# Adding up a state space model's states one step later on TensorE

## The chip, the cores and the metric

The kernel runs on one core of one Trainium2 chip. Five engines of that core work side by side, each through its own queue in order: TensorE (PE in the profile, with PEld for its weight loads), VectorE (DVE), ScalarE (ACT), GpSimd (POOL) and SyncE (SP). ACT, SP and POOL also issue DMAs from their queues. Engines wait for each other on semaphores. The metric is the device time in microseconds of one execution; lower is better. Before the change the median of six runs was 1602.23 us (1597.44 to 1605.59).

## The reference, cut to what matters

Two layers act on 8 sequences of 512 tokens with 128 channels. Each layer is `x + s * silu(g)`, where `s` and `g` are two models that read the same normalised input and don't need each other. In the first layer `s` is a state space model and `g` a mixture of 24 experts; in the second `s` is an attention with 8 heads and `g` a mixture of 128 experts.

The part that matters here is the state space model:

```
deltaA  = exp(dt[..., None] * A)                 # A: 256 channels x 16 states
deltaBx = dt[..., None] * Bm[:, :, None, :] * x[..., None]
h = dA * h + dBx                                  # over the 512 tokens
y = einsum('bdn,bn->bd', h, C)                    # added up over the 16 states
y = (y + x * D) * silu(z)
```

and beside it the first mixture: 24 experts of 128 to 512 to 128 channels, with a normalisation of the summed hidden rows between the two products.

## The kernel before, in words

Everything is in fp32. A sequence of the state space model (`b`, eight of them) has its 256 channels in two halves of 128 partitions and its 512 tokens along the free axis. `front(b)` makes the inputs (convolution, `dt`, `B`, `C`) in two pieces; `scan(b, ...)` goes through the 16 states two at a time, so a sequence has 8 steps and the model 64; `back(b, yt)` does the output projection and a small MLP in three pieces.

One step of `scan` does the following for its two states (lines 597 to 636). ACT issues two DMAs that spread `B` and `C` over the partitions (`bb`, `cb`, lines 600 and 601, two buffers each). For each half, ACT makes `da = exp(dt * A)` for two states (line 606, two buffers), DVE multiplies `u = bb * dx` for both states at once (line 608), runs two scans along the tokens in place (line 610), and multiplies by `cb` (line 611). The tile `u` has four buffers, so two steps' worth. Then PE adds the states up: sixteen transposes by the identity (line 632) accumulate the two halves' two states, four token tiles each, into `py`, a PSUM tile with one buffer that lasts the whole sequence. A sequence's `py` is opened at its first step by the products of the `x * D` term (line 621), and the previous sequence's `py` is read just before by `gated` on DVE (`yt = py * zs`, line 652), which `turn()` calls.

The model is a Python generator that yields after each step; other parts of the program call `step()` to place the next step between their own pieces. One step stands ahead of the first mixture. The mixture has three stages. In `expert1(e)` (24 times) POOL gathers an expert's rows in three chunks, PE transposes them (line 450), ACT copies them out, PE adds a bias product and the expert's product (lines 456 and 457), ACT scales the result out of PSUM (line 458), and SP stores it. `between()` (16 times) gathers the pairs of hidden rows, sums and normalises them, mostly on POOL, DVE and ACT, and folds the attention's weights on PE beside it. `expert2(e)` (24 times) gathers again, transposes (line 521), and multiplies back to 128 channels (lines 524 and 526). A counter `due` spreads 11, 6 and 14 steps of the model over these three stages: it grows by 11/24, 6/16 or 14/24 after each piece, and a step is placed whenever it exceeds 0.5. The remaining 32 steps stand beside the attention of the second layer for sequences 0 to 5, 28 of them spread evenly over its 48 heads. After that come the last heads and the second mixture, without the model.

This is the order in which the program is written. Each engine's own queue is not quite in this order: the framework plans the order of every queue when the program is built, from its own estimate of when inputs are ready, and an earlier line goes first among those that it takes to be ready. On the chip a queue's order is fixed, and an instruction whose input is late holds everything behind it on its engine. `follows(later, earlier)` (line 119) adds an edge for this planning that says which of two instructions on one engine goes first; it costs no instruction and no semaphore.

Of the kernel before, what the change touches and what calls it, by code (L numbers as in the profile page):

```python
# [8 lines left out]
F32 = mybir.dt.float32  # L9
# [11 lines left out]
P = 128  # L21
B, L, D = 8, 512, 128
NJ = L // P
NTOK = B * L
NTT = NTOK // P
DI, DS, DTR, DFF = 256, 16, 8, 512
# [3 lines left out]
CP = 128  # L30
# [17 lines left out]
def tile_kernel(ctx: ExitStack, tc: tile.TileContext, t: dict, out: bass.AP):  # L48
    nc = tc.nc
    V, S, G, T, Q = nc.vector, nc.scalar, nc.gpsimd, nc.tensor, nc.sync  # L50
# [11 lines left out]
    ident = const.tile([P, P], F32, name="ident")  # L62
# [36 lines left out]
    def bc(ap, shape):  # L99
        return ap.to_broadcast(list(shape))  # L100
# [48 lines left out]
    def pool(stack, name, bufs, side, **more):  # L149
        return stack.enter_context(tc.tile_pool(name=name, bufs=bufs, side=side, **more))  # L150
# [6 lines left out]
    ps_y = pool(ssm, "ps_y", 1, "left", space=PSUM)  # L157
# [184 lines left out]
    ddiag = w0.tile([P, 2, P], F32, name="ddiag")  # L342
# [100 lines left out]
    def expert1(e, w):  # L443

        we = w(e)
        px = ps_e.tile([P, SLOTS], F32, name="px", tag="pe")
        for c, r in enumerate(SROWS):
            xg = me.tile([CP, D], F32, name="xg", bufs=8)
            gather(xg[:r], xn_dram, inv[:r, c, e : e + 1])
            T.transpose(px[:, c * CP : c * CP + r], xg[:r], ident[:r, :r])  # L450
        xT = me.tile([P, SLOTS], F32, name="xTe", tag="xTe")
        S.copy(xT, px)
        hs = me.tile([CP, SG, DH], F32, name="hs", tag="big", bufs=4)
        for c, r in enumerate(SROWS):
            ph = ps_e.tile([CP, DH], F32, name="ph", tag="pe")
            T.matmul(ph[:r], chosen(e, r), bias[:, 0:DH], start=True, stop=False)
            T.matmul(ph[:r], xT[:, c * CP : c * CP + r], we, start=False, stop=True)
            S.activation(hs[:r, c, :], ph[:r], AF.Copy, scale=wsl[:r, c, e : e + 1])
        store(hs_dram, e, hs)

    def between():

# [49 lines left out]
    def expert2(e, w):  # L512
        we = w(e)
        po = ps_e.tile([CP, SG, D], F32, name="po", tag="pe")
        os = me.tile([CP, SG, D], F32, name="os", tag="o")
        hg = me.tile([CP, SG, DH], F32, name="hg", tag="big", bufs=4)
        for c, r in enumerate(SROWS):
            gather(hg[:r, c, :], hid_dram, inv[:r, c, e : e + 1])
            pt = ps_e.tile([P, NJ, CP], F32, name="pht", tag="pe")
            for f in range(NJ):  # L520
                T.transpose(pt[:, f, :r], hg[:r, c, f * P : (f + 1) * P], ident[:r, :r])  # L521
            hT = me.tile([P, NJ, CP], F32, name="hgT", tag="xTe")
            S.activation(hT[:, :, :r], pt[:, :, :r], AF.Relu)  # L523
            T.matmul(po[:r, c, :], chosen(e, r), bias[:, DH:], start=True, stop=False)
            for f in range(NJ):
                T.matmul(po[:r, c, :], hT[:, f, :r], we[:, f, :], start=False, stop=(f == NJ - 1))  # L526
            S.activation(os[:r, c, :], po[:r, c, :], AF.Copy, scale=wsl[:r, c, e : e + 1])
        store(os_dram, e, os)

    def fetch(b):  # L530

# [59 lines left out]

    NC = 2

    def scan(b, xs, dt, dx, turn):


        for n0 in range(0, DS, NC):
            bb = ms.tile([P, NC, L], F32, name="bb")
            cb = ms.tile([P, NC, L], F32, name="cb")
            S.dma_start(bb, xd_dram[b][DTR + n0 : DTR + n0 + NC, :].partition_broadcast(P))  # L600
            S.dma_start(cb, xd_dram[b][DTR + DS + n0 : DTR + DS + n0 + NC, :].partition_broadcast(P))
            us = []
            for hf in range(2):
                da = ms.tile([P, NC, L], F32, name="da")
                for j in range(NC):
                    S.activation(da[:, j, :], dt[:, hf, :], AF.Exp, scale=a_neg[:, hf, n0 + j : n0 + j + 1])  # L606
                u = ms.tile([P, NC, L], F32, name="u", bufs=4)
                V.tensor_tensor(u, bb, bc(dx[:, hf : hf + 1, :], (P, NC, L)), ALU.mult)  # L608
                for j in range(NC):
                    V.tensor_tensor_scan(u[:, j, :], da[:, j, :], u[:, j, :], 0.0, ALU.mult, ALU.add)  # L610
                V.tensor_tensor(u, u, cb, ALU.mult)  # L611
                us.append(u)
            if n0 == 0:
                turn()

                py = ps_y.tile([P, NJ, DI], F32, name="py")
                for i in range(NJ):
                    for hf in range(2):  # L620
                        m = T.matmul(
                            py[:, i, hf * P : (hf + 1) * P], xs[:, hf, i * P : (i + 1) * P], ddiag[:, hf, :],
                            start=(i % 2 == 0 and hf == 0), stop=False, skip_group_check=True,
                        )
                        if i % 2 == 0 and hf == 0:
                            first = m
                        else:
                            follows(m, first)
            for hf in range(2):
                for j in range(NC):  # L630
                    for i in range(NJ):
                        T.matmul(  # L632
                            py[:, i, hf * P : (hf + 1) * P], us[hf][:, j, i * P : (i + 1) * P], ident,
                            is_transpose=True, start=False, stop=(n0 + j == DS - 1), skip_group_check=True,
                        )
            yield py

    def gate(xT):

# [368 lines left out]
    def step():  # L1008

        nonlocal taken  # L1010
        if taken < NSTEP:
            next(model_steps)
            taken += 1

    def model():


        for state in front(0):
            pass
        ending = iter(())  # L1020
        py = zs = None
        for b in range(B):
            xT, xs, dt, dx = state
            yts = []

            def turn():
                if b > 0:
                    yts.append(gated(py, zs))

            coming = front(b + 1) if b + 1 < B else iter(())  # L1030
            steps_b = scan(b, xs, dt, dx, turn)
# [11 lines left out]
            py, zs = pyb, zsb  # L1043
        for _ in back(B - 1, gated(py, zs)):
            pass

    NSTEP = B * DS // NC
    model_steps = model()
    taken = 0


    def mixture():
        w = weights((P, DH), t["W1"])
        for e in range(E0):
            expert1(e, w)
            yield 11, E0
        w = weights((P, NJ, D), t["W2"])
        w(0)
        for _ in between():
            yield 6, NTT // 2  # L1060
        for e in range(E0):
            expert2(e, w)
            yield 14, E0
# [3 lines left out]
    for n, of in mixture():  # L1067
        due += n / of
        while due > 0.5:
            step()  # L1070
            due -= 1.0
    moe.close()


# [56 lines left out]
    last = Attention(at, m_qk, w_vo, (ps_x, "px"), (ps_q, "pq"), (ps_s, "ps"), (ps_t, "pt"), (ps_o, "po"))  # L1131
# [95 lines left out]
```

## Time and profile before

| what | us |
|---|---|
| median of six runs | 1602.23 |
| the profiled execution, whole | 1593.88 |
| its span in the profile | 1592.2 |
| busy in the span: DVE | 1242.6 |
| busy in the span: PE | 1232.8 |
| busy in the span: ACT | 975.4 |
| busy in the span: POOL | 603.8 |
| PE's transposes of the states, line 632: busy | 165.2 (1024 of them, 302 ns each) |
| PE idle just before them, until a state's last product on DVE | 127.3 |

The stages follow each other in time, and in the profiled execution they lie about so: the first experts' stage from 95 to 288 us, the stage between from 288 to 433, the second experts' stage from 433 to 653, the turn to the second layer up to 742, attention beside the model up to 1323, and the rest.

Busy times are read against the span of a stage, not of the whole: an engine with the same share over the whole span can be full in one stage and nearly idle in another. An idle time in the profile is put down to the instruction in front of which the engine sat, and to what ended it. `PEclk` is the clock granted to TensorE as a share of the full one.

### The profile page before, as it was taken

The page shows a single profiled execution, that of the slowest core. Times are in us where ns is not written, and L with a number is a line of the kernel's source. Part 1 is how long each engine was busy: PE and PEld are TensorE (multiplying, and loading weights), DVE is VectorE, ACT ScalarE, POOL GpSimd, SP SyncE. Part 2 cuts the span into 40 slices and gives each one's busy share as a digit, 9 for nine tenths or more (in the row PEclk, how much of TensorE's full clock was granted, in tenths as well). Part 3 has the DMA queues.
Part 4 walks back from the last instruction along what each step waited for, and adds up shares of the span by engine and source line. Part 5 has one row for each costly group of instructions (what it writes and reads, how often), then busy time and mean ns, then how long its engine had stood idle before and what let it go on. Part 6 is the DMA issues. An engine that isn't in the chain of part 4 may idle for free.

```text
span 1592.2 us, 20596 instructions
## 1 busy us (share of the span) xinstructions
PE 1232.8 (77%) x6793; PEld 869.3 (55%) x6793; DVE 1242.6 (78%) x2759; ACT 975.4 (61%) x1726; POOL 603.8 (38%) x504
## 2 busy tenths in 40 slices
PE   6888889322579888547878989989889898899854
PEld 4644455222367776524556656766557576467533
DVE  5639775698946858769999999999899996465454
ACT  5146667577747677456766858667587675542442
POOL 1247552665154443573503560043260402010455
PEclk9679999655689999877989999999999999999886
DMA  6556767787467765533222342133122210538233
GB/s 192 176 183 217 265 217 240 241 259 232 166 200 222 240 186 170 145 61 108 56 90 70 80 113 62 54 100 80 61 65 64 79 48 14 138 109 237 57 106 96
DMA packets 170669, 218.84 MB, mean 137 GB/s; under 512 B 16618, under 2 KB 118074, under 8 KB 170562
## 3 DMA queue, kind: packets, MB, share of 16 engines
q1 hardware_dynamic: 126018, 99.39, 20.3%
q10 hardware_dynamic: 18432, 67.12, 12.8%
q0 software_dynamic: 26112, 51.01, 12.4%
q8 instruction: 54, 0.88, 0.2%
q14 instruction: 53, 0.43, 0.1%
HBM read 161.56 MB, written 55.84 MB: 137 GB/s over the span
## 4 chain that ended last, share of the span: by engine, by line
DVE 38%; PE 30%; DMA 8%; issue 8%; ACT 7%; POOL 6%; another core or an unknown queue 2%; SPq 1%; DVEq 0%; ACTq 0%; POOLq 0%
DVE u L610 11%; DVE u L611 5%; PE po L886 4%; PE sc L859 4%; DVE u L608 4%; DVE sc L861 3%; POOL o L131 3%; PE py L632 2%; PE pp L879 2%; PE po L526 2%; DVE s L897 2%; POOL hd L128 2%; DMA cb<-xd_dram 2%; DMA hd<-hs_dram,row 2%
## 5 line engine op out<-in xcount | busy, mean ns | idle before, releaser
L610 DVE TENSOR_TENSOR_SCAN u<-da,u 128x512 f32<-128x512 f32 x256 | 311.8, 1239 | 60.4 <-ACT da L606 35.8
L632 PE MATMUL py<-ident,u 128*128 128x128 f32 x1024 | 165.2, 302 | 127.4 <-DVE u L611 127.3
L632 PEld LDWEIGHTS py<-ident,u 128*128 128x128 f32 x1024 | 132.5, 156 | 170.2 <-DVE u L611 152.7
L886 PE MATMUL po<-v,pT 128*128 128x129 f32 x1280 | 186.0, 288 | 33.1 <-DVE s L897 15.5
L886 PEld LDWEIGHTS po<-v,pT 128*128 128x128 f32 x1280 | 167.8, 200 | 63.4 <-issue 26.9
L606 ACT ACTIVATE da<-dt,a_neg 128x512 f32<-128x512 f32 x256 | 176.3, 719 | 38.5 <-DVE u L610 35.0
L865 ACT ACTIVATE prob<-sc,mn 128x128 f32<-128x128 f32 (+3 forms) x256 | 130.0, 527 | 106.7 <-DVE mn L861 73.4
L859 PE MATMUL sc<-xaT,qm 128*128 128x128 f32 (+3 forms) x512 | 179.5, 460 | 13.8 <-ACT prob L865 10.2
L608 DVE TENSOR_TENSOR u<-bb,lp 128x1024 f32<-128x1024 f32 x128 | 156.0, 1238 | 8.9 <-DMA bb<-xd_dram 8.8
L611 DVE TENSOR_TENSOR u<-u,cb 128x1024 f32<-128x1024 f32 x128 | 157.6, 1231 | 1.0
L861 DVE CUSTOM_DVE_ANT_0 sc<-sc,mask 128x128 f32<-128x128 f32 (+3 forms) x256 | 124.3, 496 | 31.7 <-PE sc L859 20.1
L131 POOL DMA_INDIRECT o<-os_dram,row x64 | 112.7, 1761 | 76.9 <-DMA bb<-xd_dram 31.7
L879 PE MATMUL pp<-ident,prob 128*128 128x128 f32 x640 | 112.7, 286 | 36.5 <-DVE pT L881 19.7
L833 POOL DMA_INDIRECT xs_dram<-xn,idx x64 | 77.4, 1210 | 160.9 <-DVE row L830 73.8
L128 POOL DMA_INDIRECT xg<-xn_dram,inv x72 | 100.2, 1391 | 91.5 <-PE px L450 41.7
L879 PEld LDWEIGHTS pp<-ident,prob 128*128 128x128 f32 x640 | 79.8, 146 | 96.5 <-issue 43.4
L128 POOL DMA_INDIRECT hg<-hid_dram,inv x72 | 89.8, 1247 | 101.0 <-PE pht L521 73.4
L859 PEld LDWEIGHTS sc<-xaT,qm 128*128 128x128 f32 x512 | 84.0, 198 | 57.1 <-ACT prob L865 25.4
L128 POOL DMA_INDIRECT hd<-hs_dram,row x64 | 79.4, 1241 | 68.0 <-DMA qkv_w<-in_qkv_w 23.7
L881 ACT COPY pT<-pp 128x384 f32<-128x384 f32 (+1 forms) x100 | 51.4, 514 | 63.9 <-PE pp L879 51.3
L526 PEld LDWEIGHTS po<-we,hgT 128*128 128x128 f32 (+1 forms) x576 | 71.7, 189 | 23.9 <-issue 19.5
L526 PE MATMUL po<-we,hgT 128*128 128x128 f32 (+1 forms) x576 | 80.6, 287 | 0.9 <-ACT hgT L523 0.8
(289 smaller groups left out, 2560.1 us busy)
## 6 DMA issues: line engine op xcount, KB each, us to landing
bb<-xd_dram ACTq DMA_DIRECT2D x64, 512.0 KB
cb<-xd_dram ACTq DMA_DIRECT2D x64, 512.0 KB
we<-in_W SPq DMA_DIRECT2D x48, 256.0 KB
hs_dram<-hs SPq DMA_DIRECT2D x24, 512.0 KB
hid_dram<-hd SPq DMA_DIRECT2D x32, 256.0 KB
we<-in_we SPq DMA_DIRECT2D x16, 512.0 KB
hs_dram<-hs SPq DMA_DIRECT2D x24, 192.0 KB
xb<-in_x SPq DMA_DIRECT2D x16, 256.0 KB
```

Source lines behind the costliest of these rows:

```text
L128: G.indirect_dma_start(dst, None, table[:, :], IOA(idx, 0))
L131: G.indirect_dma_start(dst, None, table[:, :], IOA(idx, 0), compute_op=ALU.add)
L526: T.matmul(po[:r, c, :], hT[:, f, :r], we[:, f, :], start=False, stop=(f == NJ - 1))
L606: S.activation(da[:, j, :], dt[:, hf, :], AF.Exp, scale=a_neg[:, hf, n0 + j : n0 + j + 1])
L608: V.tensor_tensor(u, bb, bc(dx[:, hf : hf + 1, :], (P, NC, L)), ALU.mult)
L610: V.tensor_tensor_scan(u[:, j, :], da[:, j, :], u[:, j, :], 0.0, ALU.mult, ALU.add)
L611: V.tensor_tensor(u, u, cb, ALU.mult)
L632: T.matmul(py[:, i, hf * P : (hf + 1) * P], us[hf][:, j, i * P : (i + 1) * P], ident, is_transpose=True, start=False, stop=(n0 + j == DS - ...
L859: T.matmul(sc[:, :w], qm[:, i * P : w], xaT[:, :w], start=True, stop=True)
L861: V.tensor_tensor_reduce(sc[:, :w], sc[:, :w], mask[:, L - w :], -1.0, FMAX, ALU.add, ALU.min, mn[:, i : i + 1])
L879: T.transpose(pp[:, c, :], prob[i][:, k * P : (k + 1) * P], ident)
L886: T.matmul(po[:, i - i0, :], pT[:, i * (i + 1) // 2 + k, :], v[:, k, hd % 4, :], start=(k == 0), stop=(k == i),)
```

## The change

A step's transposes are no longer issued with the step. `scan` yields the step's four states' tiles (`us`), the model keeps them as `waiting`, and the transposes are written in the next step, behind that step's instructions on ACT and DVE. With them the turn of a sequence moves: `gated`, the products of the `x * D` term (now `skipped`) and the three pieces of `back` stand in steps 1, 2 and 3 of the following sequence and no longer in steps 0, 1 and 2. The last step's transposes stand behind the loop.

In the two experts' stages a list `ahead` holds the last product of the expert written last, and each transpose gets an edge that places it behind that product on PE. In the stage between, and from the second layer on, the list is empty.

```diff
@@ expert1
-            T.matmul(ph[:r], xT[:, c * CP : c * CP + r], we, start=False, stop=True)
+            m = T.matmul(ph[:r], xT[:, c * CP : c * CP + r], we, start=False, stop=True)
             S.activation(hs[:r, c, :], ph[:r], AF.Copy, scale=wsl[:r, c, e : e + 1])
         store(hs_dram, e, hs)
+        ahead[:] = [m]
@@ expert2
-                T.matmul(po[:r, c, :], hT[:, f, :r], we[:, f, :], start=False, stop=(f == NJ - 1))
+                m = T.matmul(po[:r, c, :], hT[:, f, :r], we[:, f, :], start=False, stop=(f == NJ - 1))
...
         store(os_dram, e, os)
+        ahead[:] = [m]
@@ scan
                 us.append(u)
-            if n0 == 0:
-                turn()
...
-            for hf in range(2):
-                for j in range(NC):
-                    for i in range(NJ):
-                        T.matmul(
-                            py[:, i, hf * P : (hf + 1) * P], us[hf][:, j, i * P : (i + 1) * P], ident,
-                            is_transpose=True, start=False, stop=(n0 + j == DS - 1), skip_group_check=True,
-                        )
-            yield py
+            yield us
+
+    def skipped(xs):
+
+        py = ps_y.tile([P, NJ, DI], F32, name="py")
...
+        return py
+
+    ahead = []
+
+    def add_up(py, us, last):
+
+        for hf in range(2):
+            for j in range(NC):
+                for i in range(NJ):
+                    m = T.matmul(
+                        py[:, i, hf * P : (hf + 1) * P], us[hf][:, j, i * P : (i + 1) * P], ident,
+                        is_transpose=True, start=False, stop=(last and j == NC - 1), skip_group_check=True,
+                    )
+                    for before in ahead:
+                        follows(m, before)
@@ model
-            for k in range(DS // NC):
-                pyb = next(steps_b)
-                if k == 0:
-                    ending = back(b - 1, yts[0]) if b > 0 else iter(())
-                if k in (0, 1, 2):
+            for k, us in enumerate(scan(b, dt, dx)):
+                if k == 1:
+                    if b > 0:
+                        ending = back(b - 1, gated(py, zs))
+                    py = skipped(xs)
+                if waiting is not None:
+                    add_up(py, waiting, k == 0)
+                waiting = us
+                if k in (1, 2, 3):
                     next(ending, None)
...
+        add_up(py, waiting, True)
         for _ in back(B - 1, gated(py, zs)):
             pass
@@ mixture: ahead.clear() ahead of between(), and after the last expert2
```

More of the change, by code (lines that the diff above doesn't have):

```diff
@@ L592, in tile_kernel, with scan @@
     NC = 2
-    def scan(b, xs, dt, dx, turn):
+    def scan(b, dt, dx):
         for n0 in range(0, DS, NC):
@@ L612, in scan @@
                 us.append(u)
-            if n0 == 0:
-                turn()
-                py = ps_y.tile([P, NJ, DI], F32, name="py")
-                for i in range(NJ):
-                    for hf in range(2):
-                        m = T.matmul(
-                            py[:, i, hf * P : (hf + 1) * P], xs[:, hf, i * P : (i + 1) * P], ddiag[:, hf, :],
-                            start=(i % 2 == 0 and hf == 0), stop=False, skip_group_check=True,
-                        )
[L625 to L629, printed above, removed]
-                for j in range(NC):
-                    for i in range(NJ):
-                        T.matmul(
-                            py[:, i, hf * P : (hf + 1) * P], us[hf][:, j, i * P : (i + 1) * P], ident,
-                            is_transpose=True, start=False, stop=(n0 + j == DS - 1), skip_group_check=True,
-                        )
-            yield py
+            yield us
[4 more added lines that the diff above has]
+                m = T.matmul(
+                    py[:, i, hf * P : (hf + 1) * P], xs[:, hf, i * P : (i + 1) * P], ddiag[:, hf, :],
+                    start=(i % 2 == 0 and hf == 0), stop=False, skip_group_check=True,
+                )
+                if i % 2 == 0 and hf == 0:
+                    first = m
+                else:
+                    follows(m, first)
+        return py
+    ahead = []
+    def add_up(py, us, last):
+        for hf in range(2):
+            for j in range(NC):
+                for i in range(NJ):
+                    m = T.matmul(
+                        py[:, i, hf * P : (hf + 1) * P], us[hf][:, j, i * P : (i + 1) * P], ident,
+                        is_transpose=True, start=False, stop=(last and j == NC - 1), skip_group_check=True,
+                    )
+                    for before in ahead:
+                        follows(m, before)
     def gate(xT):
@@ L1020, in model @@
         ending = iter(())
-        py = zs = None
+        py = zs = waiting = None
         for b in range(B):
             xT, xs, dt, dx = state
[L1024 to L1028, printed above, removed]
             coming = front(b + 1) if b + 1 < B else iter(())
-            steps_b = scan(b, xs, dt, dx, turn)
-            for k in range(DS // NC):
-                pyb = next(steps_b)
-                if k == 0:
-                    ending = back(b - 1, yts[0]) if b > 0 else iter(())
-                if k in (0, 1, 2):
+            for k, us in enumerate(scan(b, dt, dx)):
[7 more added lines that the diff above has]
+                if k in (1, 2, 3):
                     next(ending, None)
@@ L1042, in model @@
                 yield
-            py, zs = pyb, zsb
+            zs = zsb
+        add_up(py, waiting, True)
         for _ in back(B - 1, gated(py, zs)):
@@ L1058, in mixture @@
         w(0)
+        ahead.clear()
         for _ in between():
@@ L1071, in tile_kernel @@
             due -= 1.0
+    ahead.clear()
     moe.close()
```

## The prediction

> **What bounds the kernel now.** I read the page's engine shares first, then the busy times cut at the stages, because the change acts in some stages only. Columns of the second table: stretch in us, its length, then PE, PEld, DVE, ACT and POOL busy with counts, granted clock, DMA share, GB/s.
>
> ```profile
> span 1592.2 us, 20596 instructions
> PE 1232.8 (77%) x6793; PEld 869.3 (55%) x6793; DVE 1242.6 (78%) x2759; ACT 975.4 (61%) x1726; POOL 603.8 (38%) x504
> ```
>
> ```profile
> 95.00:288.00 193.00, 160.74 (x642) 87.89 (x641) 138.92 (x131) 124.58 (x207) 107.10 (x80) 0.94 0.73 236
> 288.00:433.00 145.00, 46.42 (x184) 36.28 (x182) 127.32 (x219) 98.38 (x174) 75.07 (x61) 0.58 0.69 220
> 433.00:653.00 220.00, 183.59 (x1340) 154.68 (x1340) 149.97 (x142) 148.93 (x284) 91.23 (x75) 0.95 0.65 201
> 653.00:742.00 89.00, 45.54 (x204) 31.66 (x204) 69.57 (x139) 40.41 (x74) 52.30 (x33) 0.69 0.40 101
> 742.00:1323.00 581.00, 515.86 (x2828) 360.12 (x2828) 559.13 (x1381) 407.92 (x706) 179.02 (x128) 0.96 0.25 72
> ```
>
> No engine is full over the whole, but stages differ. In both experts' stages (first and third row) PE is the busiest: 160.7 of 193 us and 183.6 of 220, 83% each, with DVE at 72% and 68%. Between them (second row) DVE leads with 88% and PE has little to do. Beside the attention (last row) DVE is full: 96%.
>
> Then I asked who PE waits for in the two experts' stages, and who DVE waits for (each first in the first stage, then in the second; us in total, times, longest).
>
> ```profile
> PE py L632 <- DVE u L611: 17.7, 15, 2.6
> ...
> PE py L632 <- DVE u L611: 19.0, 17, 2.1
> ...
> DVE u L610 <- ACT da L606: 9.8, 4, 3.4
> ...
> DVE u L610 <- ACT da L606: 25.5, 11, 7.0
> ```
>
> PE's largest wait in each is for DVE, in front of the transposes, about 1.1 us at a time. DVE in turn waits for ACT's `da`. The order of instructions in time shows why both hold (PE, then DVE):
>
> ```profile
> 190.72 1.05 PE L456 MATMUL ph<-bias,pick 96*128 96x512 bf16 x3
> 194.39 1.63 PE L632 MATMUL py<-ident,u 128*128 128x128 f32 x8 [2.62 <-DVE u L611]
> 196.82 1.97 PE L632 MATMUL py<-ident,u 128*128 128x128 f32 x8 [0.80 <-DVE u L611]
> 198.57 4.25 PE L457 MATMUL ph<-we,xTe 128*128 128x512 f32 x6
> ...
> 205.96 1.23 DVE L610 TENSOR_TENSOR_SCAN u<-da,u 128x512 f32<-128x512 f32 x1 [6.92 <-issue]
> ```
>
> It is a ring. PE stands at 191.8 in front of transposes whose states DVE finishes at 196.8; the next expert's product is behind them and starts at 198.6. ACT's queue has that product's copy out of PSUM next, sits idle 5.84 us until 200.5, and comes to the next `da` at 205.2. DVE, which needs it, has sat idle for 6.92. A late state costs PE, then ACT, then the next state.
>
> **The change part by part.** The sum is made against the profiled execution: span 1592.2, whole 1593.9, that is 1.7 outside the span. The median shown is 1602.2, 8.3 above it; I take the same difference off both.
>
> Work: none is added or removed. There are still 1024 transposes (8 in 1.04 us at the full clock, so 2.1 us a step), eight openings of `py` (16 records in 1.95 us each) and eight `yt` (1.21 us). The edges are no instructions.
>
> 1. The wait for DVE in the experts' stages goes. A transpose written one step later stands a step, some 15 us (220 / 14), after the place where it waits today, where the wait is 2.6 us at most. So 17.7 + 19.0 = 36.7 us of PE's idle time go, the upper bound of this part's gain. What is late next is ACT's copies and the gathers: PE already waits 5.7 us for the row copies (`xTe`) in the first stage and 8.8 for `os` in the second. The lower bound is nothing: other waits take it all. I take the share that PE reaches where it is best fed for long, the attention's row: 515.86 / 581 = 88.8%. At that share the stages take 160.74 / 0.888 = 181.0 and 183.59 / 0.888 = 206.8 us, so 12.0 and 13.2 less: 25.2. DVE allows it: 138.9 of 181 is 77%.
>
> 2. The clock. PE at half the clock is part of the loss above: the window from 195 to 201 us was granted 0.50 where the ten before 194 had 1.00, and the six products at 198.57 took 4.25 us where six take 2.84 at the full clock. If such spells go too, their half is won. By the rows near transposes' waits (195 to 201 and 212 to 215 us, 0.50 both) it is 4.5 us in the first stage. I keep it for the low end. [...]
>
> 3. A new wait, on DVE. `u` has four buffers, so a step's first product (line 608) needs the transposes of the step two earlier. These now stand behind the expert in front of the step in between. I laid this on the old times: the end of that expert's last product plus 1.04 us, against the start of line 608. In the first stage the buffers come 3.7 to 16 us early, but once 2.0 late. In the second stage they would come late by 26.6, 6.4, 8.8 and 6.7 us in its first four steps, and by 5.0 in three later ones; all in all 55.4 us, the upper bound. Behind line 608 on DVE's queue are the scans and `front`'s and `back`'s products, and ACT waits for those. What covers it is DVE's own idle time in that stage, 220 - 150 = 70 us, and that a step needs 10.7 us of DVE (150 / 14) in 15.7. The lower bound is nothing. Nearest is the only wait that line 608 has in that stage, for its DMA: 6.7 us in six waits. I take 6.7 as the loss. [...]
>
> 4. Between the stages PE's long waits (63.5 us between 300 and 400 us) go, and are worth nothing: PE is busy 46 of 145 us there, DVE 88%, and DVE's waits are for the gathered rows. ACT did sit idle once, 10.6 us, behind such a wait (`m_qk`); if that is on the path, 10.6 are won. I take 0.
>
> 5. The turn of a sequence one step later. Moved with it are `yt` on DVE, the opening on PE, `back`'s products on PE, its ACT work, its load `xnb` and its store `s_dram` on SP (8 each), and its bias sum on POOL (line 702). SP's queue has no compute behind it, and POOL is busy 38%. A store is some 20 us later beside the attention; the sum that reads it is asked for right behind the last moved piece for sequence 6 only, and POOL, not DVE, waits there. Taken as 0. `py` has one buffer, so nothing of a sequence can be added up before `yt` is read, and `yt` now stands behind two steps' states on DVE. PE waits for it 11.3 us in three turns today. Taken as unchanged.
>
> 6. Beside the attention PE's wait for the states is not among its seven largest, and DVE is at 96%. Nothing to win; 0.
>
> Sum: 1602.2 - 25.2 + 6.7 = 1583.7 (the profiled execution: 1575).
>
> **The rivals.**
> More than that: all 36.7 us and the clock's 4.5 come back, no new wait: 1561. For it: the ring multiplies a late state. Against it: 88.8% is the best that PE reaches anywhere for long.
>
> The gain is hidden: PE waits at the same places for copies and gathers, DVE meets the attention with the same work left: 1602. For it: DVE's states run without a gap from 114 to 158 us, so PE's lead there buys nothing until DVE has caught up. Against it: DVE idles 54 and 70 us in the two stages, 17 and 33 of them by name behind ACT, which waits for PE.
>
> Slower, by part 3: line 608 waits for its buffer at the head of the second experts' stage, and `da` and the copies on ACT wait for DVE. If 70% of the 55.4 stay, +38.8 - 25.2 = +13.6: 1616. It decides from 25.2 of 55.4, that is 45%.
>
> Slower, by part 5: at the three turns beside the attention (steps 40, 48, 56) DVE has no states to work on until `yt`, opening and transposes are through. A step's transposes there end up to 17.9 us after its states (states of step 48 end at 1002.9, transposes at 1020.8); half of three such waits is 26.9 against the 18.5 won: 1611. It decides from 6.2 us a turn. Against it: heads fill DVE meanwhile.
>
> **How the numbers follow.** Forecast 0.46 (its own range 1571 to 1595), more than that 0.11, hidden 0.15, buffers 0.17, turns 0.11. So faster 0.57, within 0.3% (5 us, about what a measurement of this kernel tells from no change) 0.15, slower 0.28. The low end is the forecast's waits in full without new ones, 1602.2 - 36.7 = 1565; the high end is just over the buffers' case, 1617. Outside I leave the rest of "more" and of the buffers' worst.
>
> **What would show it.** Right: PE's wait for line 611 in front of the transposes near 0 in both experts' stages, PE's share there near 89%, the stages 12 and 13 us shorter, the attention's stage within 8 us of 581. Part 3 wrong: DVE waiting for PE's transposes in front of line 608 by more than 25 us. Part 5 wrong: DVE under 95% beside the attention, with gaps after steps 40, 48 and 56. Most likely to break the forecast: the planner orders all queues anew, and gives back in the attention what the experts' stages win.

## The result and the profile after

The changed kernel took 1614.1 us (median of 20 runs, 1601.4 to 1623.1), the kernel before 1601.2 us on the same chip (46 runs): a ratio of 1.0078, interval 1.0063 to 1.0093. It became slower; forecast was 1584, faster. Chips differ more than that: in the comparisons of this study, each made on one chip, the kernel before took 1600 or 1601 us twice and 1567 to 1574 us four times. So ratios are compared below, and stage times only between chips of the same kind. The profiled execution of the kernel before was one of its faster ones, so its span and the changed kernel's lie 20.6 us apart where the medians lie 12.9 apart.

The page's first lines of the changed kernel:

```profile
span 1612.8 us, 20605 instructions
...
PE 1231.9 (76%) x6793; PEld 866.0 (54%) x6793; DVE 1236.4 (77%) x2747; ACT 992.7 (62%) x1746; POOL 609.4 (38%) x504
```

The work is what it was: PE and DVE, the two engines that bound the stages, are busy for no longer than before (1232.8 and 1242.6); ACT is by 17 us (eight more loads of its function tables, 197 of 1.28 us each, make 10 of them) and POOL by 6. What was lost is idle time. To see where, I cut both executions at the same events, not at round numbers: the first gather of the second experts' stage (`hg`), the last product of its last expert (`po`), the first score product of the attention (`sc`), the end.

| stretch, us | before | after | difference | forecast |
|---|---|---|---|---|
| up to the second experts' stage | 437.3 | 433.1 | -4.2 | -12.0 |
| second experts' stage | 209.9 | 219.9 | +10.0 | -6.5 |
| turn to the second layer | 94.9 | 104.0 | +9.1 | 0 |
| attention and the rest | 850.1 | 855.9 | +5.8 | 0 |

The same cut in the profile of the kernel before (second stage, turn) and in that of the changed kernel (columns as in the prediction: stretch, length, PE, PEld, DVE, ACT, POOL busy with counts, granted clock, DMA share, GB/s; the first row of the changed kernel is the round one shown of before):

```profile
437.30:647.20 209.90, 177.37 (x1305) 149.37 (x1303) 140.31 (x133) 142.26 (x274) 91.23 (x75) 0.96 0.64 197
647.20:742.10 94.90, 49.22 (x221) 34.57 (x221) 75.43 (x144) 43.49 (x79) 52.40 (x33) 0.69 0.43 111
```

```profile
95.00:288.00 193.00, 160.26 (x628) 84.72 (x626) 139.80 (x130) 124.79 (x206) 107.65 (x78) 0.93 0.72 233
433.10:653.00 219.90, 187.45 (x1339) 157.05 (x1340) 142.37 (x141) 147.54 (x280) 100.54 (x76) 0.92 0.62 190
653.00:757.00 104.00, 48.53 (x237) 35.14 (x235) 76.80 (x143) 46.98 (x83) 58.50 (x36) 0.69 0.38 97
757.00:1351.40 594.40, 523.47 (x2877) 364.62 (x2876) 558.06 (x1385) 424.01 (x726) 169.86 (x124) 0.96 0.25 70
```

PE's share in the second experts' stage is 85%, no more than before (84.5%) and not the 89% of the forecast, and DVE's is 65%. Who DVE waits for in that stage, and then in the turn (us in total, times, longest):

```profile
DVE u L609 <- PE py L640: 60.2, 9, 25.0
...
DVE lno_st L107 <- DMA o<-os_dram,row: 24.9, 11, 7.1
```

Lines have moved by one or more: 609 is the product `u = bb * dx`, 611 the scan, 612 the product by `cb`, 640 the transposes. The first of the two lines was not there at all before; in its place stood DVE's 25.5 us for `da`. The second was half as long, in the turn of before:

```profile
DVE lno_st L107 <- DMA o<-os_dram,row: 12.2, 4, 7.2
```

The longest of the new waits, in order of time (start, duration, engine, line, operation, and in brackets the idle time ahead of it and what ended it), first PE, then DVE:

```profile
447.14 1.11 PE L527 MATMUL po<-we,hgT 128*128 128x128 f32 x8
448.09 0.83 PE L708 MATMUL pr<-w,hT 128*128 128x128 f32 x6
455.79 0.27 PE L525 MATMUL po<-bias,pick 96*96 96x128 bf16 x1 [6.86 <-ACT os L528]
455.85 1.96 PE L527 MATMUL po<-we,hgT 128*96 128x128 f32 x8
457.60 3.62 PE L640 MATMUL py<-ident,u 128*128 128x128 f32 x16
```

```profile
433.45 1.13 DVE L673 SCALAR_TENSOR_TENSOR zm<-zm,rms_ss,n1w 128x128 f32<-128x128 f32 x4
459.56 1.23 DVE L609 TENSOR_TENSOR u<-bb,lp 128x1024 f32<-128x1024 f32 x1 [24.97 <-PE py L640]
```

The four buffers of `u` are full. The states in the buffer that DVE wants were finished at 416.4 us, but their transposes stand behind the expert's last product on PE, that product behind one that waits 6.86 us for ACT's copy, and DVE runs nothing at all from 434.6 to 459.6. In these rows both engines keep their order: on PE the transposes come at 457.60, behind the product that waited 6.86 us, though their first states were done 41.2 us earlier, and on DVE nothing runs in the 24.97 us until the waiting product does. after_again, the same kernel on another chip, has DVE's instructions in the same order there, with 16.41 us in that place.

### The profile page after: what moved, and what is told of

Its sections match the earlier page's. It is cut to its first block, busy times and chain, and to the rows that moved or that the text cites. A ratio compares the mean times of both kernels' runs of the same rounds, so it can differ in the third digit from the quotient of the medians.

```text
span 1612.8 us, 20605 instructions
## 1 busy us (share of the span) xinstructions
PE 1231.9 (76%) x6793; PEld 866.0 (54%) x6793; DVE 1236.4 (77%) x2747; ACT 992.7 (62%) x1746; POOL 609.4 (38%) x504
## 4 chain that ended last, share of the span: by engine, by line
PE 31%; DVE 30%; POOL 10%; DMA 10%; ACT 9%; issue 8%; another core or an unknown queue 1%; SPq 1%; ACTq 0%; POOLq 0%; DVEq 0%
DVE u L611 8%; POOL o L131 4%; PE po L895 4%; PE sc L868 4%; DVE u L612 3%; DVE u L609 3%; DVE sc L870 3%; POOL hd L128 2%; PE py L640 2%; PE po L527 2%; PE pp L888 2%; PE ph L457 2%; PE pv L853 2%; DVE s L906 1%; PE pc L566 1%
## 5 line engine op out<-in xcount | busy, mean ns | idle before, releaser
L895 PE MATMUL po<-v,pT 128*128 128x129 f32 x1280 | 184.7, 288 | 30.9 <-DVE s L906 11.7
L640 PE MATMUL py<-ident,u 128*128 128x128 f32 x1024 | 148.1, 292 | 68.7 <-DVE u L612 68.7
L868 PE MATMUL sc<-xaT,qm 128*128 128x128 f32 (+3 forms) x512 | 180.2, 460 | 17.7 <-ACT prob L874 14.1
L640 PEld LDWEIGHTS py<-ident,u 128*128 128x128 f32 x1024 | 128.2, 151 | 90.6 <-DVE u L612 75.2
L128 POOL DMA_INDIRECT hg<-hid_dram,inv x72 | 97.0, 1348 | 118.4 <-PE pht L522 73.2
L890 ACT COPY pT<-pp 128x384 f32<-128x384 f32 (+1 forms) x108 | 55.8, 517 | 47.5 <-PE pp L888 42.8
```

Of the source, the lines that this page charges most:

```text
L640: m = T.matmul(py[:, i, hf * P : (hf + 1) * P], us[hf][:, j, i * P : (i + 1) * P], ident, is_transpose=True, start=False, stop=(last and j ...
L868: T.matmul(sc[:, :w], qm[:, i * P : w], xaT[:, :w], start=True, stop=True)
L895: T.matmul(po[:, i - i0, :], pT[:, i * (i + 1) // 2 + k, :], v[:, k, hd % 4, :], start=(k == 0), stop=(k == i),)
```

## The experiments

Three theories were set against each other. A: deferral and edges are each harmless, but both together hold the four buffers of `u` too long, and DVE waits. B: the deferral is what lengthens the turn and the attention. C: every edit makes the planner order all queues anew, and what falls out costs or gains some us by itself.

What came out of all runs, cut as above. "Wait" is DVE's wait in front of the product `u` for the transposes, in the second experts' stage. The last column is the run's ratio to the kernel before on the same chip.

| run | second stage | wait | turn | attention and rest | ratio, interval |
|---|---|---|---|---|---|
| chips where before takes 1600 us: | | | | | |
| before | 209.9 | 0 | 94.9 | 850.1 | 1 |
| after | 219.9 | 60.2 | 104.0 | 855.9 | 1.0078, 1.0063 to 1.0093 |
| late4 | 215.5 | 39.7 | 101.4 | 854.8 | 1.0048, 1.0025 to 1.0071 |
| late16 | 204.1 | 11.7 | 105.0 | 857.2 | 0.9966, 0.9934 to 0.9998 |
| late19 | 206.0 | 6.3 | 96.3 | 853.2 | 0.9855, 0.9810 to 0.9900 |
| chips where it takes 1567 to 1574 us: | | | | | |
| after_again | 211.5 | 50.8 | 104.3 | 837.5 | 1.0108, 1.0071 to 1.0144 |
| exp_only | 213.6 | 53.0 | 104.3 | 864.8 | 1.0293, 1.0258 to 1.0327 |
| att_only | 204.1 | 0 | 95.9 | 828.8 | 0.9986, 0.9962 to 1.0010 |
| all_free | 195.2 | 5.5 | 95.9 | 830.2 | 0.9884, 0.9848 to 0.9920 |
| edges_only | 186.6 | 0 | 95.3 | 834.2 | 0.9897, 0.9837 to 0.9956 |
| edge2 | 202.9 | 36.7 | 104.4 | 838.9 | 1.0023, 0.9996 to 1.0050 |
| bufs4_small | 205.2 | 26.9 | 103.7 | 840.1 | 1.0043, 1.0022 to 1.0063 |
| bufs6_small | 200.5 | 0 | 97.7 | 830.9 | 0.9932, 0.9908 to 0.9957 |
| bufs5_small | 206.1 | 24.2 | 103.7 | 849.1 | 1.0198, 1.0153 to 1.0244 |
| one_back | 209.6 | 24.0 | 102.9 | 837.2 | 1.0040, 1.0006 to 1.0074 |
| tail_free | 204.6 | 38.2 | 101.1 | 840.9 | 1.0058, 1.0030 to 1.0085 |
| edge1 | 198.5 | 7.0 | 99.5 | 841.9 | 1.0026, 0.9991 to 1.0061 |
| mixed | 197.9 | 0 | 95.4 | 828.7 | 0.9945, 0.9924 to 0.9966 |
| turn_fixed | 212.8 | 52.1 | 97.5 | 847.3 | 1.0118, 1.0074 to 1.0162 |

The kernel before was not profiled on the faster chips. att_only stands for it there: up to the end of the second experts' stage its queues are those of the kernel before, and the stage takes 204.1 us. Three runs with the changed kernel's queues up to that point (after_again, exp_only, turn_fixed) take 211.5 to 213.6 us, so the stage lost 7 to 10 us on both kinds of chip.

### The parts of the change, each alone

Where the model goes the way of before in a range of sequences, each step's transposes follow at once (`late` says which sequences are deferred; at the seam the held states are added up and the list of edges is cleared):

```diff
-                if k == 1:
+                late = b < 4            # exp_only; att_only: b >= 4; edges_only: False
+                if k == (1 if late else 0):
...
-                if waiting is not None:
-                    add_up(py, waiting, k == 0)
-                waiting = us
-                if k in (1, 2, 3):
+                if late:
+                    if waiting is not None:
+                        add_up(py, waiting, k == 0)
+                    waiting = us
...
+                else:
+                    add_up(py, us, k == DS // NC - 1)
+                if k - late in (0, 1, 2):
```

exp_only has deferral and edges in the first 32 steps alone, those beside the experts:

> The transposes stand a step later, with their edges, in the first 32 steps only (the first mixture); from step 32 on everything is as before, the turn of a sequence too. Theory A (the buffers: DVE waits in front of a step's first product until the transposes behind an expert are through, 60 us in the second experts' stage): half of the loss or more is here, +6 to +13 us against the kernel before, and the wait of 50 us or more is still there. Theory B (the later turn and the later transposes beside the attention): 0 to +5 us. Theory C (any new plan of the queues costs some): no order, within 15 us of before.

att_only has the deferral from step 32 on, and no edges (both lines `ahead[:] = [m]` are out):

> As before in the first 32 steps, a step later from step 32 on, no edges. Theory A: within 5 us of the kernel before. Theory B: +8 to +15 us, with the first attention scores some 9 us later after the last expert, and DVE near 94% beside the attention. Theory C: no order, within 15 us.

all_free is the change without those two lines, so deferral everywhere and no edge:

> The change without its edges: transposes a step later everywhere, but placed by the planner. Theory A: DVE's wait for its buffers falls from 64 us to under 20, and the time falls to that of the kernel before or up to 10 us under it. Theory B: still +8 to +15 us. Theory C: no order.

edges_only has the edges and no deferral:

> The kernel before with the edges alone: a step's transposes stay in their step but stand behind the last product of the expert written last. Theory A: the buffers come one step earlier than with the change, DVE waits for them under 15 us, PE waits for the states as before (30 to 40 us in the two experts' stages), and the time is within 5 us of before. Theory B: within 3 us. Theory C: up to 15 us either way.

Measured: exp_only 1.0293, att_only 0.9986, all_free 0.9884, edges_only 0.9897. Theory B falls with att_only: the turn of a sequence one step later, and the deferral beside the attention, cost nothing that can be measured. Each half of the change alone is a gain, of 15 to 18 us on a kernel of 1574 us, about the forecast's 18.5; that is more than theory A gave them (up to 10 and up to 5 us). Only both together lose. That exp_only loses nearly three times as much as the whole change is more than the buffers explain, since its wait and its stage are after_again's; its attention and rest take 864.8 us, 27 more than after_again's, and DVE waits 25.0 us for gathers in front of `lno_st` beside the attention, where the changed kernel's profile (after) has 13.2. Beside the attention its program is that of the kernel before, but the order into which its queues fell is not; that this order is what costs the 27 us is likely, and not shown.

### Buffers

The pool of `u` had no room for more buffers, so other tiles got fewer, the same in all three runs:

```diff
-                u = ms.tile([P, NC, L], F32, name="u", bufs=4)
+                u = ms.tile([P, NC, L], F32, name="u", bufs=6)   # 4, 5 or 6
...
-        xb = xp.tile([P, NJ, D], F32, name="xb", bufs=6)
+        xb = xp.tile([P, NJ, D], F32, name="xb", bufs=2)
# likewise we 4 to 3, xg 8 to 6, lw and lb to 1, v 3 to 2
```

> The changed kernel as it is, on the chip of its companions. Both theories: 0.6 to 1.0% over the kernel before, the second experts' stage near 220 us, DVE waiting some 60 us in it for transposes.

> The changed kernel with six buffers for u, three steps' worth. For the room, loads and expert weights have fewer buffers (xb 2, we 3, xg 6, lw and lb 1, v 2); bufs4_small is the same with four buffers for u and is what this is to be held against. Theory A (it is the buffers): DVE's wait in front of a step's first product falls under 10 us, the second experts' stage falls to 185 to 200 us, the turn behind it to 95, and the time is 20 to 40 us under bufs4_small. Theory C (new plans cost some, whatever they are): within 15 us of bufs4_small.

> The changed kernel with the fewer buffers of bufs6_small and four for u: the control. Both theories: like the changed kernel or up to 10 us slower, with its wait of 50 to 65 us.

> The changed kernel with five buffers of u, in the room that the runs with four (1.0043) and six (0.9932) had, their other sizes. Theory A, a dose: the DVE's wait in front of the product of u by B, behind the transposes, lies between the 61 us with four and none with six, at 15 to 40 us, and the second experts' stage at 200 to 205 us; time 0.996 to 1.002. If two buffers more are worth 17 us by an order of the queues that happened to come out and not by the wait: anything from 0.99 to 1.01, and no relation between that wait and the stage's time.

after_again repeats the loss on a faster chip, with a smaller wait and a shorter stage than the 60 and 220 us expected. With four buffers and the small sizes the ratio is 1.0043, with six 0.9932: 17 us for two buffers, between what the theories gave (20 to 40 for A, at most 15 for C), and DVE's wait for the transposes in the stage is gone. But the stage itself shortens by 4.7 us only, because DVE's wait for `da` takes its place (3.9 us with four buffers, 37.8 with six); the other 15 us come in the turn (6.0) and in the attention and the rest (9.2). Five buffers are a miss for A: the wait is where it was expected, 24.2 us, but the kernel is the slowest of the three, 1.0198, again through the attention and the rest, 849.1. So the number of buffers moves two things, and one of them isn't the wait.

### One stage, one end, one expert less

```diff
# edge2: edges in the second experts' stage only; edge1: in the first only
# one_back: behind the expert before the last
-        ahead[:] = [m]
+        ahead[:] = last[-1:]
+        last.append(m)
# tail_free, in expert2
-        ahead[:] = [m]
+        ahead[:] = [m] if e < 19 else []
# mixed: deferral without edges up to step 11, then edges without deferral
# up to step 31, the way of before after that
+                late = b * DS // NC + k < 12
```

> The change without its edges in the first experts' stage: a step later everywhere, edges in the second experts' stage alone. Theory A: the buffers' wait lies in the second stage, so this is like the changed kernel: that stage 212 to 222 us, the turn some 104, the time 5 to 20 us over the kernel before. Theory C: no order.

> The change with one thing less strict: the transposes stand behind the last product of the expert before the one given last, not behind the one given last. Theory A (u's four buffers are held by transposes that come one step late and then stand behind an expert as well): most of the second half of the holding goes. The DVE's wait in front of the product of u by B, behind the transposes, falls from 55 to 64 us to under 20 us, the second experts' stage from 211 us to 190 to 200, the turn behind it from 104 us to 95 to 98, the time to 0.985 to 0.993 of the kernel before. Theory C (any new order of the queues costs this much, the buffers are a bystander): the wait may fall, but the time stays at 1.00 to 1.01.

> The change, with the edges left out behind the last five experts of the second layer's experts' stage; everything else as in the change. If the longer turn and the longer attention come from steps that are held back at that stage's end (theory B): the turn is 95 to 98 us and not 104, the attention 590 us or less, the time 8 to 15 us under the changed kernel, 0.995 to 1.003 of the kernel before. If they come from the holding of buffers earlier in the stage (theory A alone): the stage shortens by no more than 5 us, the turn stays at 103 to 105 us, and the time is 1.005 to 1.012.

> One half of the change in each experts' stage: in the first, a step's transposes one step later without the edges; in the second, the edges without the deferral; beside the attention the kernel before's way. Theory A (each half alone is a gain, both on four buffers are the loss): first experts' stage 178 to 183 us, second 186 to 196 us, no wait of the DVE for transposes in front of the product of u by B over 10 us, turn 95 to 98 us, time 0.983 to 0.991 of the kernel before. Theory C (gains and losses come from whichever order of the queues falls out): anything from 0.985 to 1.02.

> Deferral everywhere, edges in the first experts' stage only. Theory A: that stage has so much idle time on the DVE that a held buffer costs little there (DVE busy 140 of 193 us): 183 to 188 us, the second stage like the one with deferral alone (193 to 198 us), turn 95 to 98 us, time 0.986 to 0.994 of the kernel before. Theory C: anything up to 1.02.

Measured: edge2 1.0023, one_back 1.0040, tail_free 1.0058, mixed 0.9945, edge1 1.0026. Theory A is right in sign for the stage wherever the wait is small (edge1 198.5 us, mixed 197.9), and mixed is a gain, though smaller than A gave (0.983 to 0.991). In edge2 the wait and the loss are smaller than expected. A fails outright twice. In one_back the wait fell to 24.0 us, a little over the bound, but the stage stayed at 209.6: DVE stands 14.4 us in front of `zm` and 12.4 us in front of `lp` there. And edge1 has hardly any wait (7.0 us), yet is 1.4% slower than all_free, from which it differs by the edges of the first stage alone: 3.6 us in the turn, 11.7 in the attention and the rest. The turn of tail_free did not come back to 95 us either, so transposes held back at the stage's end aren't the whole of the longer turn.

What does go with the turn is the order of DVE's queue behind the stage. The changed kernel, in the turn:

```profile
678.78 0.49 DVE L107 BATCH_NORM_STATS2 lno_st<-o 128x6 f32<-128x128 f32 x2 [5.24 <-DMA o<-os_dram,row]
...
680.67 0.29 DVE L107 BATCH_NORM_STATS2 lno_st<-o 128x6 f32<-128x128 f32 x1 [1.33 <-DMA o<-os_dram,row]
...
682.49 0.29 DVE L107 BATCH_NORM_STATS2 lno_st<-o 128x6 f32<-128x128 f32 x1 [1.44 <-DMA o<-os_dram,row]
...
689.94 0.29 DVE L107 BATCH_NORM_STATS2 lno_st<-o 128x6 f32<-128x128 f32 x1 [7.08 <-DMA o<-os_dram,row]
...
695.43 0.29 DVE L107 BATCH_NORM_STATS2 lno_st<-o 128x6 f32<-128x128 f32 x1 [1.46 <-DMA o<-os_dram,row]
...
695.92 1.19 DVE L609 TENSOR_TENSOR u<-bb,lp 128x1024 f32<-128x1024 f32 x1
```

Eight `lno_st`, the statistics of gathered experts' outputs for two sequences, stand in a row; seven waits for gathers lie in front of them, and no step of the model lies between them. In late19 (the last of these sections), which has the order of all_free, four come, with DVE's steps among them:

```profile
657.98 0.29 DVE L107 BATCH_NORM_STATS2 lno_st<-o 128x6 f32<-128x128 f32 x1 [0.22 <-DMA o<-os_dram,row]
658.19 1.21 DVE L612 TENSOR_TENSOR u<-u,cb 128x1024 f32<-128x1024 f32 x1
...
664.29 0.29 DVE L107 BATCH_NORM_STATS2 lno_st<-o 128x6 f32<-128x128 f32 x1 [3.09 <-DMA o<-os_dram,row]
664.50 0.17 DVE L108 BATCH_NORM_AGGREGATE lno_mv<-lno_st 128x2 f32<-128x6 f32 x1
664.58 1.19 DVE L609 TENSOR_TENSOR u<-bb,lp 128x1024 f32<-128x1024 f32 x1
```

Read over all runs: the seven with eight in a row (after, after_again, edge2, one_back, bufs4_small, late4, late16) have turns of 101.4 to 105.0 us. The six with the order of before (edges_only, mixed and before itself) or of all_free (att_only, late19) have 94.9 to 96.3. The others have orders of their own and lie between, 97.5 to 101.1, with bufs5_small and exp_only at 104. From the end of the second stage to the end of the kernel the four with eight in a row on the faster chips (after_again, edge2, one_back, bufs4_small) take 940.1 to 943.8 us, whatever their waits in the stage; the four with the order of before or of all_free (all_free itself, att_only, edges_only, mixed) take 924.1 to 929.5. So the order goes with some 16 us.

### The order of the turn alone

turn_fixed is the changed kernel with one edge on DVE, which puts the second four `lno_st` behind the attention input's statistics:

```diff
+            m = V.bn_stats(st[:, j, :], src[:, j, :])
+            if tag == "lno":
+                for before in turned:
+                    follows(m, before)
+            if tag == "ln1":
+                turned[:] = [m] if not past else []
```

> The changed kernel with one edge more, on the DVE alone: the statistics of the second sequence's experts' outputs (four lno_st) come behind those of the first sequence's attention input (ln1_st), as they stand in the kernel before's queue; in the changed kernel eight lno_st stand one behind the other. The experts' stages keep their queues and their waits. If the longer turn comes from that order of the DVE's queue: the turn falls from 104 us to 95 to 98 us, with less of the DVE's wait in front of lno_st in the turn (25 us to under 15), and the time is 6 to 12 us under the changed kernel, 1.000 to 1.005 of the kernel before. If it comes from the half step that is done earlier, before the stage's end, and is missing as work for the turn: the turn stays at 101 to 105 us, the time at 1.005 to 1.012.

The turn fell from 104.3 to 97.5 us and its waits for gathers from 26.0 to 15.8, nearly as the first reading said. The time did not: 1.0118. Attention and rest rose from 837.5 to 847.3 us, because the edge changed the order behind it as well. So the order of the queue made this turn longer, but a turn repaired by itself isn't a kernel repaired.

### Stage and order apart

Nearly every edit so far changed both. These three leave out the edges behind the first experts of the second stage (`e >= 16`, `e >= 19` in the others):

```diff
-        ahead[:] = [m]
+        ahead[:] = [m] if e >= 4 else []
```

> The changed kernel with the edges left out behind the first four experts of the second layer's experts' stage. The order of the DVE's queue behind that stage stays as it is in the changed kernel, so this run changes the stage alone. The longest of the new waits (25 us at the stage's start on the first chip, 16 us on the second) lies there. If the wait for u's buffers is what the stage loses: the stage falls from 211 us to 200 to 206 us, the turn stays at 103 to 105 us, the time is 1.002 to 1.008 of the kernel before (the change: 1.008 to 1.011). If the wait only stands in idle time of the DVE: stage 209 to 213 us, time 1.008 to 1.013.

> The same with the edges left out behind the first sixteen experts of that stage, so that eight have them; behind the stage the DVE's queue still has the changed kernel's order. If the wait is what the stage loses: stage 195 to 202 us, the DVE's wait for transposes in it under 20 us, turn 103 to 105 us, attention and rest together some 8 us longer than with deferral alone, time 0.998 to 1.004. If the wait only stands in idle time: stage 208 to 213 us, time 1.006 to 1.013.

> Three experts less with edges than in the run before it (nineteen without, five with). By this small step the DVE's queue behind the stage falls into the order that deferral alone has: four lno_st, then the other sequence's statistics, not eight in a row. If that order is the rest of the loss: the turn falls from 104 us to 95 to 98 us, attention and rest together by 6 to 10 us, and the time lies 12 to 18 us under the run before it, 0.987 to 0.994 of the kernel before. If the order is a bystander: turn 102 us or more, time within 5 us of the run before it.

Behind the stage all five queues of late16 are the changed kernel's, entry for entry. The wait went from 60.2 to 11.7 us and the stage from 219.9 to 204.1, 15.8 us, while the turn stayed at 105.0 and attention and rest at 857.2. The median follows: 0.9966 against 1.0078, or 18 us. late4's wait and stage lie between (39.7 and 215.5), and so does its ratio. The stages expected in us came from the faster chips; the differences are what compares: late4's stage is 4.4 us shorter than the changed kernel's, where 5 to 11 were given, and late16's ratio is a little better than its 0.998. Leaving out edges also changes PE's order within the stage, so these are the edges' whole effect there; that it comes by the wait rests on the two falling together. The two stretches of late16 (stage, turn), with DVE's waits for `u`'s buffers in the stage:

```profile
435.10:639.20 204.10, 178.08 (x1315) 150.38 (x1315) 144.26 (x141) 145.49 (x279) 110.10 (x76) 0.95 0.66 205
639.20:744.20 105.00, 48.94 (x237) 35.85 (x234) 76.72 (x142) 47.03 (x83) 61.23 (x36) 0.69 0.37 94
```

```profile
DVE u L609 <- PE py L640: 11.7, 3, 6.0
```

late19 takes three experts more from the edges. By the ratios (0.9855 against 0.9966) it is some 18 us faster, give or take 9 by the two intervals, and its stage is no shorter (206.0):

```profile
429.80:635.80 206.00, 182.02 (x1314) 153.64 (x1314) 141.91 (x139) 145.57 (x279) 102.78 (x76) 0.93 0.65 201
635.80:732.10 96.30, 49.83 (x236) 35.55 (x235) 76.20 (x143) 45.88 (x82) 52.69 (x33) 0.70 0.40 100
```

```profile
DVE lno_st L107 <- DMA o<-os_dram,row: 16.0, 6, 7.1
```

What differs is the queue behind the stage: the turn is 8.7 us shorter (96.3), its waits for gathers fell from 26.9 to 16.0 us, attention and rest are 4.0 us shorter, and DVE's waits in front of `lno_st` outside the turn fell from 12.9 to 0.6 us. That is 12.7 of the 16.0 us between the two profiled executions; the stage took 1.9 back, and another 5.3 lie ahead of it, where both have the same queues, so they are chance. The turn came as expected; the attention and the rest gave less (4.0 where 6 to 10 were given).

So theory A holds for the stage in sign, theory C for what lies behind it, and in late16 and late19 the two are of a size. late19 is also the fastest version: 0.9855 of the kernel before, with all_free (0.9884) and edges_only (0.9897) within its interval.

## Why the prediction was wrong

Part 1, the wait of PE, 25.2 us: right in mechanism and near in size for the whole kernel. PE's waits for the states in the second stage fell from 19.0 us to 11.8 in all_free, 5.3 in edges_only and 3.0 in late19, and these three versions are 18.4, 14.9 and 20.4 us faster (medians). late19 is not the change itself; it is the version that keeps the deferral and has little of both later losses. The way to the size is less sound. PE works in late19 at 182.02 / 206.00 = 88.4% of the second stage, against 88.8% taken from the attention's row. But that is only 3.9 us less than before at the same cuts (209.9 us; the forecast's 206.8 started from the round stretch of 220), because PE's busy time there rose too, from 177.4 to 182.0 us. And the two profiled executions lie only 6.7 us apart, so they don't show where the rest of the 20.4 us is won. In the changed kernel itself the first stage went no faster: PE's waits for the states fell from 17.7 to 3.1 us there, but others rose: for the copies `hs` from 2.9 to 7.0, for the gathers `xg` from 0.8 to 6.4, for `yt` from none to 5.0. The start of the second stage is only 4.2 us earlier, of 12.0 forecast.

Part 2, the clock, taken as nothing: right for the first stage, 0.93 granted, 0.94 before. In the second it fell from 0.96 to 0.92 at the same cuts, and PE was busy for 187.5 us, not 177.4, with 34 products more; no run separates the clock's share of that.

Part 3, the wait of DVE for `u`'s buffers, is the first term that failed, and by its size. The upper bound was good: 55.4 us laid on the old times (2.0 of them in the first stage), 60.2 measured in the second, with the longest at the head of the stage as the old times had it. The choice of 6.7 was not: it was the price of another wait of the same line, for a DMA, which says nothing about a ring through PE. The cover named, DVE's own 70 us of idle time, was real but partial: DVE's other waits did shrink (for `da` from 25.5 to 1.0 us), yet 48.5 us less of waiting in late16 shortened the stage by 15.8 us, while DVE's other waits in it grew from 16.3 to 46.8 us. That is a third; in late4 it is a fifth (4.4 of 20.5 us), and with six buffers for four a sixth (4.7 of 26.9). The bound from the old times was the row of the very operation, and a sixth to a third of it would have made 9 to 18. Counting all 55.4 would have been far too much, because DVE had waited elsewhere before.

Part 4, between the stages, taken as 0: not settled. The two stretches ahead of the second stage shift against each other from run to run, and no run separates them. Taken together they did get shorter: with the changed kernel's queues up to there the second stage starts at 429.2 to 435.1 us in four executions (after, late4, late16, late19) against 437.3 before, and on the faster chips at 430.5 to 435.4 in four (after_again, exp_only, tail_free, turn_fixed) against att_only's 446.5.

Part 5, the turn of a sequence one step later, taken as unchanged: right. att_only has it three times beside the attention and is at 0.9986.

The second term that failed, and the larger, has no part of its own and was taken as 0 with part 6: what a new order of the queues does behind the experts' stages. The text named it as most likely to break the forecast and gave it neither a price nor a chance. late16 against late19 puts it at 18 us by the ratios and about 13 by the profiled stretches, the runs on the faster chips at 16: the turn to the second layer, some 9 us, where seven waits for gathers stand in a row, and idle DVE beside the attention. By the prediction's own list of signs DVE under 95% there (93.9%) would have spoken for part 5, but the largest part of its idle time stands in front of `lno_st`, 13.2 us, not behind the turns at steps 40, 48 and 56.

From the forecast, 18.5 us faster, to the result, 12.9 us slower, it is 31.4 us. By these sizes about 18 are the order, 9 the buffers (15.8 for 6.7) and 5 part 1 (20.4 for 25.2). That they add up is no further evidence: late16 and late19 lie between the changed kernel and the one before, so the differences close by themselves. The rival "slower, by part 3" came out at its 1616 by the ratio (1602.2 × 1.0078 = 1614.7), but by luck: the wait costs 15.8 us, below the 25.2 from which it decides, and the rest is the order. By these sizes the change without the new order would have stayed a gain of some 5 us.

What stays open: why the planner's order behind the stage turns with an edge more or less. It does not simply go with the wait: late16 has eight `lno_st` in a row with 11.7 us of it, tail_free and exp_only don't have them with 38.2 and 53.0, and edge1, with 7.0, still has a turn of 99.5 us. And no run says which entry of the queue costs the attention and the rest their 4 to 10 us.

## What to carry to other kernels

Moving a consumer later keeps its input buffers for as long, so count buffers in steps: a deferral by a step and an edge behind an expert used up two steps' worth of `u`, and either alone was a gain of about 1% where both were a loss of 1%. When the trace of before lets a new wait be laid out wait by wait, price it from that layout, as a share of it, and not by the nearest other wait. Where a program's queues are ordered by a planner, the new order can be worth as much as the edit itself, as here (some 18 us between late16 and late19, against the 15.8 us that the second stage lost by the edges late16 leaves out); look for a variant that keeps the queue behind the edited stage as it was before believing either.

## What was not expected of the hardware

late16 and late19 have the same queues on every engine up to the second experts' stage. Their first experts' stage, from its first gather to the first of the next stage, took 187.2 and 178.1 us in the profiled executions, with waits for the same things in other amounts; from 95 to 275 us PE has 592 and 613 instructions there, 149.1 and 154.4 us busy. Six other executions with these queues up to there (after, late4, after_again, exp_only, tail_free, turn_fixed) took 184.8 to 187.7, so most agree within 3 us, and one can still be off by 9. The whole time of one kernel on one chip spreads by 0.6 to 1.7% where there are ten runs or more. The chips themselves spread more than the change: 1567 to 1601 us for the same kernel.
